# The inverse standard deviation of every LayerNorm taken from ScalarE and VectorE and given to GpSimd as a power of -0.5

## The chip, the cores and the metric

The kernel runs on one core of a Trainium2 chip. The metric is the time of one launch on the device in microseconds (us); of the kernel before, three runs were timed. One further execution was taken with the hardware profiler, and every duration below is from that one. The engines are named as in the profile: PE is TensorE (the matrix unit; PEld is its loading of weights), DVE is VectorE, ACT is ScalarE, POOL is GpSimd, and SP is SyncE, which only issues DMAs here. POOL issues DMAs too, from the same queue of instructions in which its arithmetic stands.

## The reference

Four graph layers over the same adjacency matrix of 3327 x 3327. Each adds its output to its input and normalizes every row of 512.

```python
def _layernorm(x, axis=-1, eps=1e-5):
    m = mean(x); v = var(x)
    return (x - m) / sqrt(v + eps)
# layers 0, 2 and 3: graph attention with 8, 8 and 4 heads (elu behind layers 2 and 3)
Wh = h @ W                                    # (n, H, D), H * D = 512
e = leaky_relu(s1[i] + s2[j], 0.2)            # s1, s2: Wh times two vectors, per head
att = softmax over j of where(adj > 0, e, -9e15)
h_prime = att @ Wh
# layer 1: mean of the first 64 neighbours, two linear layers with leaky_relu, added
x = _layernorm(x + layer(x, adj))             # four times
```

What matters here is the last line: 3327 rows of 512 are normalized four times, and no scale or shift follows.

## The kernel before

Rows are cut into 26 tiles of 128 (the last one has 127 rows, and `valid` zeroes its surplus row). A tile lies with a row on each partition, so the mean and variance of its rows are a column of 128 numbers, and the factors of a LayerNorm are computed on tiles of 128x1 or 128x2 elements.

`norm_rows` (L146) does one LayerNorm for one or two tiles. DVE computes statistics (`bn_stats` L152, `bn_aggr` L153), giving mean and variance in `mv`. ACT takes the square root of the variance plus `eps` into `rs[:, :, 0]` (L154), DVE takes its reciprocal (L155) and, at L158, makes minus the mean times it into `rs[:, :, 1]`. ACT then applies both in one pass over the 512 columns (L161). ACT evaluates functions from a table that holds some of them at a time; where the next function is in another set, an `ACT_TABLE_LOAD` stands ahead of it. The profile writes this load under the line of the instruction that needs it. The kernel's other functions on ACT are the exponential (L189, L278, L318, L1442, L1499), the sigmoid (L413) and plain copies and scalings.

`finish_steps` (L165) is the end of an attention layer for two tiles, cut into steps so that a caller can spread them: load the sums `h` from DRAM (buffer `hd`) and the layer's input `xr`, divide by the softmax's denominator (`divide`, L182), for layers 2 and 3 the elu (exponential L189 on ACT, L197 and L198 on DVE, which also add `xr`), and then `norm_rows`. In `load`, `h` goes by the queue that the caller names, and `xr` by POOL's; the DMAs of both have line 126, in `load_tile`.

The launch passes through these stages, in order of time:

- projection of layer 0 and building of the adjacency mask, to about 160 us; attention of layer 0, to about 950 (matmuls L855 and L811, DVE L833, ACT L834). The last groups of layer 0's LayerNorm overlap the next stage.
- layer 1, called sage, from about 950 to 1607 us. Its first part (L1185 to L1203) normalizes layer 0's output tile by tile and multiplies by the two weight matrices; weight tiles `wn` and `wl` come by POOL's queue, and L1193 is the first matmul that uses `wn`. Its second part accumulates neighbours' sums (L1295, 1352 matmuls) and, for each finished tile, runs `output` (L1270): a load `xi` by POOL (L1272), three DVE operations, `norm_rows` for this one tile, a store, and the projection for layer 2 (transposition L267, matmuls L277, exponential L278). POOL also issues the loads of counts `cy` (L1123).
- attention of layer 2, to about 2398 us, by the same code as layer 0.
- `third` (L1331), about 2398 to 2541 us: layer 2's finish, groups of two tiles, together with the projection for layer 3. A group's loads are issued three groups ahead; the first two loaded here take `h` by POOL, the others by SP. A tile's output is stored to `x3` by SP, transposed (L267), copied by ACT (L268) and multiplied (L277). In the middle of it come layer 3's preparation (L315 on DVE, L318 on ACT, transposition L324) and pieces of layer 2's sums (stores `hd`, loads `pes` L967). POOL clears two buffers, `sden` (L254) and `sm` (L256), for layer 3.
- attention of layer 3, first half of the rows (2541 to 2866 us), then second half (2868 to 3211 us), each in four units (matmuls L470, DVE L408, ACT L413). The second half carries the finish of the first half's 13 tiles as background jobs, by `finish_steps`, and a finish of its own that is written out apart: statistics into `mv`, a square root over seven tiles at once in `slots` (L1488), the factors in `scale` (L1470 reciprocal, L1471 product), applied by ACT (L1477) or DVE (L1479), then the store (L133).
- a tail, 3211 to 3229 us, with the last two groups of four and two tiles: the loop at L1523 to L1530 takes square roots at L1526 and calls `scale` for the group before.

PE's instructions run in the order in which the program writes them. The order of the other engines' and queues' instructions is chosen by a scheduler from a cost model, save for instructions that are wrapped in `keep_in_program_order`, which stay in written order relative to each other. So a change of the operation can also move other instructions on an engine. [...]

Of the kernel before, what the change touches and what calls it, by code (L numbers as in the profile page):

```python
# [7 lines left out]
F32 = mybir.dt.float32  # L8
# [4 lines left out]
AF = mybir.ActivationFunctionType  # L13
ALU = mybir.AluOpType
# [4 lines left out]
P = 128  # L19
LN_EPS = 1e-5  # L20
# [12 lines left out]
def kernel(  # L33
# [10 lines left out]
    nc = tc.nc  # L44
# [21 lines left out]
    const = ctx.enter_context(tc.tile_pool(name="const", bufs=1))  # L66
# [15 lines left out]
    for g in range(4):  # L82
# [6 lines left out]
    nc.gpsimd.memset(onecol[:, 31:32], 1.0)  # L89
    below0 = const.tile([P, 1], F32, name="below0")  # L90
    nc.gpsimd.memset(below0, -200.0)
    eps = const.tile([P, 1], F32, name="eps")
    nc.gpsimd.memset(eps, LN_EPS)
    valid = const.tile([P, 1], F32, name="valid")
    nc.gpsimd.memset(valid, 1.0)
    nc.gpsimd.affine_select(out=valid, in_=valid, compare_op=ALU.is_gt, fill=0.0, base=LAST,
                            pattern=[[0, 1]], channel_multiplier=-1)

    c1 = const.tile([P, 2, 16], F32, name="c1")
    c1a = const.tile([P, 2, 4], F32, name="c1a")  # L100
    iv = ident.rearrange("p (x c) -> p x c", c=8)
# [17 lines left out]
    def load_tile(dst, src, t, eng):  # L119

        if src.shape[0] == N and t == NT - 1 and LAST < P:
            nc.gpsimd.memset(dst, 0.0)
            for a, z in _row_pieces(LAST):
                eng.dma_start(out=dst[a:z, :], in_=src[t * P + a:t * P + z, :])
        else:
            eng.dma_start(out=dst, in_=src[t * P:(t + 1) * P, :])
# [16 lines left out]
            eng.dma_start(out=t[:, :, e, :FW], in_=src[:, e * FW:(e + 1) * FW].rearrange("(c p) m -> p c m", p=P))  # L143


    def norm_rows(pool, ys, t0):  # L146
        n = len(ys)
        st = pool.tile([P, 4, 6], F32, name="st")
        mv = pool.tile([P, 4, 2], F32, name="mv")
        rs = pool.tile([P, 4, 2], F32, name="rs")  # L150
        for s, y in enumerate(ys):
            nc.vector.bn_stats(out=st[:, s, :], in_=y)  # L152
            nc.vector.bn_aggr(out=mv[:, s, :], in_=st[:, s, :])  # L153
        nc.scalar.activation(rs[:, :n, 0], mv[:, :n, 1], AF.Sqrt, bias=eps)  # L154
        nc.vector.reciprocal(rs[:, :n, 0], rs[:, :n, 0])  # L155
        if t0 + n == NT:
            nc.vector.tensor_tensor(rs[:, n - 1, 0:1], rs[:, n - 1, 0:1], valid, op=ALU.mult)
        nc.vector.scalar_tensor_tensor(rs[:, :n, 1], mv[:, :n, 0], -1.0, rs[:, :n, 0],  # L158
                                       op0=ALU.mult, op1=ALU.mult)
        for s, y in enumerate(ys):  # L160
            nc.scalar.activation(y, y, AF.Identity, bias=rs[:, s, 1:2], scale=rs[:, s, 0:1])  # L161
# [3 lines left out]
    def finish_steps(pool, xin, layer, t0, n, hbufs=6, eng=nc.sync, xbufs=None, xpool=None, ebufs=None, pinned=False,  # L165
                     together=False):
        H, D = layer.H, layer.D
        ys, xs, steps = [], [], []

        def load():  # L170
            for t in range(t0, t0 + n):
                xr = xpool.tile([P, F], F32, name="xr", tag="hb") if xpool else \
                    pool.tile([P, F], F32, name="xr", bufs=xbufs)
                h = pool.tile([P, F], F32, name="h", bufs=hbufs)
                load_tile(h, hd, t, eng)
                ys.append(h)
                load_tile(xr, xin, t, nc.gpsimd)
                xs.append(xr)

        def divide(s):  # L180
            h = ys[s]
            ins = nc.vector.tensor_tensor(h.rearrange("p (h d) -> p h d", h=H), h.rearrange("p (h d) -> p h d", h=H),  # L182
                                          rec[:, t0 + s, :H].rearrange("p (h e) -> p h e", e=1).to_broadcast([P, H, D]),
                                          op=ALU.mult)
            if pinned and t0 > 2:
                tc.keep_in_program_order(ins)
            if layer.elu:
                e = pool.tile([P, F], F32, name="e", bufs=ebufs)
                ins = nc.scalar.activation(e, h, AF.Exp)  # L189
                if pinned and layer.li == 2 and (t0, s) == (2, 0):  # L190
                    tc.keep_in_program_order(ins)
                xs.append(e)

        def add(s):
            h, xr = ys[s], xs[s]
            if layer.elu:
                nc.vector.scalar_tensor_tensor(xr, xs[n + s], 1.0, xr, op0=ALU.min, op1=ALU.add)  # L197
                nc.vector.scalar_tensor_tensor(h, h, 0.0, xr, op0=ALU.max, op1=ALU.add)  # L198
            else:
                nc.vector.tensor_tensor(h, h, xr, op=ALU.add)  # L200

        steps.append(load)
        if pinned or together:
            steps += [lambda s=s: divide(s) for s in range(n)] + [lambda s=s: add(s) for s in range(n)]
        else:
            for s in range(n):
                steps += [lambda s=s: divide(s), lambda s=s: add(s)]
        steps.append(lambda: norm_rows(pool, ys, t0))
        return ys, steps

# [1120 lines left out]
    def third(first):  # L1331
        with tc.tile_pool(name="col3", bufs=1) as cp:
# [5 lines left out]
            with tc.tile_pool(name="p_w", bufs=1, reuse_waits="tile") as wp, \  # L1338
# [23 lines left out]
                for t0 in range(0, NT, 2):  # L1362
# [4 lines left out]
                    for s, y in enumerate(ys):  # L1367
                        t = t0 + s
# [22 lines left out]
            with tc.tile_pool(name="f3", bufs=2) as fp, tc.tile_pool(name="f4", bufs=1) as gp:  # L1391
                g = gp.tile([P, HALF, F], F32, name="g")
                st = gp.tile([P, HALF, 2, 6], F32, name="st4")
                mv = gp.tile([P, HALF, 2], F32, name="mv4")
                rs = gp.tile([P, HALF, 2], F32, name="rs4")
# [71 lines left out]
                def scale(q0, n, keep, every):  # L1467
                    def factors():
                        qs = slice(q0, q0 + n)
                        keep(nc.vector.reciprocal(rs[:, qs, 0], rs[:, qs, 0]))  # L1470
                        keep(nc.vector.scalar_tensor_tensor(rs[:, qs, 1], mv[:, qs, 0], -1.0, rs[:, qs, 0],  # L1471
                                                            op0=ALU.mult, op1=ALU.mult))

                    def one(q):
                        y = g[:, q, :]
                        if q % every == 1:
                            keep(nc.scalar.activation(y, y, AF.Identity, bias=rs[:, q, 1:2], scale=rs[:, q, 0:1]))  # L1477
                        else:
                            keep(nc.vector.tensor_scalar(y, y, rs[:, q, 0:1], rs[:, q, 1:2], op0=ALU.mult, op1=ALU.add))  # L1479
                        store(y, HALF + q, q)  # L1480

                    return [factors] + [lambda q=q: one(q) for q in range(q0, q0 + n)]

                def slots(q0, n, pt, e):
                    keep = tc.keep_in_program_order if e == 1 else lambda ins: ins
                    qs = slice(q0, q0 + n)
                    if e == 2:
                        return [lambda: nc.scalar.activation(rs[:, qs, 0], mv[:, qs, 1], AF.Sqrt, bias=eps)] + \  # L1488
                            scale(q0, n, keep, 3)
                    y = g[:, qs, (NS - 1) * P:]  # L1490
                    h = fp.tile([P, 4, P], F32, name="h", bufs=2)
# [31 lines left out]
                for k, (q0, n, parts) in enumerate(lasts):  # L1523
                    for f in parts[2:]:
                        f()
                    keep(nc.scalar.activation(rs[:, q0:q0 + n, 0], mv[:, q0:q0 + n, 1], AF.Sqrt, bias=eps))  # L1526
                    if k > 0:
                        for f in scale(*lasts[k - 1][:2], keep, 2):
                            f()
# [191 lines left out]
```

## Time and profile before

| | |
|---|---|
| three runs | 3236.37, 3238.24, 3240.77 us |
| median | 3238.24 us |
| profiled execution, own time | 3230.94 us |
| its span, first to last instruction | 3229.1 us |
| PE busy, share | 3137.4 us, 97% |
| DVE busy, share | 2626.5 us, 81% |
| ACT busy, share | 2295.1 us, 71% |
| POOL busy, share | 266.6 us, 8% |
| table loads at L154 | 45, 57.7 us |
| square roots at L154 | 59, 17.4 us |
| reciprocals at L155 | 59, mean 0.163 us |

The shares are of the span. A group's row in the profile gives the line, the engine, the operation, the tiles it writes and reads, how often it ran, its busy time and the mean length of one, and then the idle time of its engine just before it with what ended most of that. A row of the timeline gives start and length, the instruction, and in brackets how long its engine had been idle before it and for what. "Granted clock" (PEclk) is the share of full speed at which PE was allowed to run; its mean over the span was 0.987.

### The profile page before, as it was taken

Reading aid. Unit: us, or ns where it says so; the run is one execution under the profiler, and the core shown is the slowest. Engines: PE = TensorE matmul, PEld = TensorE weight load, DVE = VectorE, ACT = ScalarE, POOL = GpSimd, SP = SyncE. Lnnn points to the kernel's source line nnn. Section 1 sums busy time; section 2 is a strip of 40 time slices with the busy share of each in tenths; the row PEclk is TensorE's granted clock in tenths of the full one; section 3 lists DMA queues with packets and bytes.
Section 4 is the critical chain, followed back from the end, with each engine's and each line's share of the span. In section 5 each row is a group of like instructions: output and inputs, shape, how many; then the busy total and the mean of one; then the engine's idle time right before and its main releaser. Section 6 shows DMA issues by size and latency. Waiting matters only on the chain. (4 is left out here: it accounts for less than half of the span.)

```text
span 3229.1 us, 44980 instructions
## 1 busy us (share of the span) xinstructions
PE 3137.4 (97%) x17910; PEld 1602.3 (50%) x17910; DVE 2626.5 (81%) x2316; ACT 2295.1 (71%) x1855; POOL 266.6 (8%) x414
## 2 busy tenths in 40 slices
PE   8899999999999999999999999999989999999997
PEld 7643343333334467777744333333347655555444
DVE  5799999999987655555499999999999666677887
ACT  1388888899883234444398988899988655568896
POOL 3110000000000111111220000000011000010110
PEclk9999999999999999999999999999999999999998
DMA  9742113111024345555441111011137211122212
GB/s 360 272 149 80 41 51 137 59 45 42 25 87 138 104 127 133 134 142 152 120 135 42 41 35 39 20 42 42 32 107 242 85 43 43 43 59 89 85 47 69
DMA packets 358321, 301.80 MB, mean 93 GB/s; under 512 B 232756, under 2 KB 291966, under 8 KB 356575
## 3 DMA queue, kind: packets, MB, share of 16 engines
q1 hardware_dynamic: 325727, 187.73, 19.9%
q0 software_dynamic: 26864, 103.50, 10.0%
q10 hardware_dynamic: 5520, 7.69, 0.7%
q8 instruction: 142, 2.33, 0.3%
q14 instruction: 68, 0.56, 0.1%
HBM read 221.97 MB, written 76.84 MB: 93 GB/s over the span
## 5 line engine op out<-in xcount | busy, mean ns | idle before, releaser
L834 ACT ACTIVATE y<-t,bi,sc 128x3328 fp8e4<-128x3328 f32 (+1 forms) x520 | 1336.9, 2604 | 100.0 <-PE pd L811 47.8
L855 PE MATMUL po<-t,vj 128*64 128x448 f32 (+1 forms) x6656 | 1272.9, 522 | 14.6 <-DVE t L833 14.5
L855 PEld LDWEIGHTS po<-t,vj 128*64 128x64 f32 x6656 | 461.0, 137 | 687.8 <-issue 617.6
L470 PE MATMUL po<-t,vj 128*128 128x448 f32 (+1 forms) x1456 | 523.3, 516 | 6.2 <-DVE ob L500 3.6
L408 DVE SCALAR_TENSOR_TENSOR t<-rba,qc,mk 128x1664 f32<-128x1664 f32 (+2 forms) x234 | 408.2, 1753 | 127.7 <-PE po L470 88.2
L413 ACT ACTIVATE y<-t,bi,sc 128x1664 fp8e4<-128x1664 f32 (+2 forms) x234 | 374.3, 1617 | 182.5 <-DVE t L408 170.8
L470 PEld LDWEIGHTS po<-t,vj 128*128 128x128 f32 x1456 | 272.1, 190 | 241.5 <-issue 149.8
L833 DVE SCALAR_TENSOR_TENSOR t<-rba,qc,mask 128x3328 f32<-128x3328 f32 (+1 forms) x130 | 381.1, 2987 | 5.7 <-PE po L855 4.9
L833 DVE SCALAR_TENSOR_TENSOR t<-rbb,qc,mask 128x3328 f32<-128x3328 f32 (+1 forms) x130 | 379.9, 2982 | 6.8 <-PE po L855 3.2
L833 DVE SCALAR_TENSOR_TENSOR t<-rbb,qc,mk 128x3328 f32<-128x3328 f32 (+1 forms) x130 | 379.2, 2981 | 6.7 <-PE po L855 4.5
L833 DVE SCALAR_TENSOR_TENSOR t<-rba,qc,mk 128x3328 f32<-128x3328 f32 (+1 forms) x130 | 379.7, 2986 | 5.7 <-PE po L855 3.4
L1295 PE MATMUL acc<-zs,kt 128*128 128x512 f32 x1352 | 360.2, 420 | 0.0
L277 PE MATMUL pw<-wsb,xT 128*128 128x264 f32 (+1 forms) x1248 | 301.7, 397 | 8.8 <-DVE vt L283 7.3
L1295 PEld LDWEIGHTS acc<-zs,kt 128*128 128x128 f32 x1352 | 256.0, 190 | 51.8 <-PE pk L1146 0.8
L811 PE MATMUL pd<-y,sden 128*32 128x384 fp8e4 (+1 forms) x3328 | 270.2, 343 | 0.0
L277 PEld LDWEIGHTS pw<-wsb,xT 128*128 128x128 f32 x1248 | 242.1, 197 | 50.9 <-issue 6.5
L1153 ACT CAST pk<-cy 128x512 f32<-128x512 bf16 x169 | 99.1, 587 | 222.6 <-DVE kt L1167 216.1
L1167 DVE SCALAR_TENSOR_TENSOR kt<-pk,mb 128x512 fp32r<-128x512 f32 x169 | 115.5, 684 | 115.4 <-PE pk L1164 114.2
L811 PEld LDWEIGHTS <-sden 128*32 128x32 bf16 x3328 | 89.1, 95 | 165.3 <-issue 149.9
L283 DVE TENSOR_TENSOR vt<-pw,dc 128x256 f32<-128x256 f32 x156 | 58.7, 417 | 70.5 <-ACT dc L278 64.7
L1193 PE MATMUL pz<-wn,xT 128*128 128x512 f32 x208 | 96.0, 605 | 5.9 <-DMA wn<-in_wnT_dram 5.5
L1123 POOL DMA_DIRECT2D cy<-ctd x91 | 68.0, 747 | 371.1 <-ACT pk L1153 304.7
(249 smaller groups left out, 2234.2 us busy)
## 6 DMA issues: line engine op xcount, KB each, us to landing
raw<-in_adjT_dram SPq DMA_DIRECT2D x67, 416.0 KB
vj<-v SPq DMA_DIRECT2D x169, 128.0 KB
cy<-ctd POOLq DMA_DIRECT2D x78, 256.0 KB, 4.3
h<-hd SPq DMA_DIRECT2D x61, 256.0 KB
v<-vt SPq DMA_DIRECT2D x50, 256.0 KB
xr<-x POOLq DMA_DIRECT2D x45, 256.0 KB, 3.2
md<-mask SPq DMA_DIRECT2D x26, 416.0 KB
mb<-md SPq DMA_DIRECT2D x169, 64.0 KB
```

Source lines behind the costliest of these rows:

```text
L277: nc.tensor.matmul(pw[e][:, :FW + H], xT[:, c, :], wsb[:, c, e, :], start=c == 0, stop=c == FC - 1)
L408: ins = nc.vector.scalar_tensor_tensor(t[:, :w], rb[:, lo:lo + w], self.qc[:, j, h:h + 1], mask_at[0](j, i0 + lo, w), op0=ALU.max, op1=ALU ...
L413: nc.scalar.activation(y[:, :w], t[:, :w], AF.Sigmoid, bias=self.bi[:, j, h:h + 1], scale=self.sc[:, j, h:h + 1], saturate=False)
L470: nc.tensor.matmul(po[c][k * D:(k + 1) * D, :z - a_], vj[:, j % 2, k * D:(k + 1) * D], ts[k][:, a_:z], start=j == 0, stop=j == NT - 1)
L811: nc.tensor.matmul(pd[c][32 * kk:32 * kk + 32, :w_], lhsT, rhs, start=(kk, c) not in seen, stop=last and j == NT - 1)
L833: nc.vector.scalar_tensor_tensor(to, ro, self.qc[:, j, h:h + 1], m, op0=ALU.max, op1=ALU.mult)
L834: nc.scalar.activation(yo, to, AF.Sigmoid, bias=self.bi[:, j, h:h + 1], scale=self.sc[:, j, h:h + 1], saturate=False)
L855: nc.tensor.matmul(po[c][k * D:(k + 1) * D, :z - a_], vj[:, j % 2, x_:x_ + D], t[:, k, a_:z], start=j == 0, stop=j == NT - 1)
L1153: nc.scalar.copy(pks[k % 2], carry[b, t // 4 * 4][:, t % 4:t % 4 + 2, :])
L1167: nc.vector.scalar_tensor_tensor(kt, pk, NEIGHBOURS, mb[:, t:t + 2, :], op0=ALU.is_le, op1=ALU.mult)
L1193: nc.tensor.matmul(pz, xT[:, c, :], wn[:, c, :], start=c == 0, stop=c == FC - 1)
L1295: nc.tensor.matmul(acc, kts[b, t][:, s * P:(s + 1) * P], zs(t, c), start=t == 0 and c == 0, stop=t == NT - 1 and c == 1)
```

## The change

A helper `rsqrt` replaces the square root on ACT and the reciprocal on DVE by two instructions on POOL: the addition of eps to the variance, and a power with the exponent -0.5, read from a constant tile `power` that takes the place of the tile `eps`. It is used at all places: in `norm_rows` (59 executions, 32 of them on 128x2 and 27 on 128x1 elements), and in the last half's own finish (128x7, 128x4 and 128x2). The roots in the tail were pinned in written order and their replacements are not. One more edit goes with it: in the finish of layer 2, within and just ahead of `third`, the loads of `xr` go by SP's queue and no longer by POOL's; there are 26 of them, of 256 KB each.

```diff
--- before.py
+++ after.py
@@ -89,13 +89,13 @@
     nc.gpsimd.memset(onecol[:, 31:32], 1.0)
     below0 = const.tile([P, 1], F32, name="below0")
     nc.gpsimd.memset(below0, -200.0)
-    eps = const.tile([P, 1], F32, name="eps")
-    nc.gpsimd.memset(eps, LN_EPS)
     valid = const.tile([P, 1], F32, name="valid")
     nc.gpsimd.memset(valid, 1.0)
     nc.gpsimd.affine_select(out=valid, in_=valid, compare_op=ALU.is_gt, fill=0.0, base=LAST,
                             pattern=[[0, 1]], channel_multiplier=-1)
 
+    power = const.tile([P, 8], F32, name="power")
+    nc.gpsimd.memset(power, -0.5)
     c1 = const.tile([P, 2, 16], F32, name="c1")
     c1a = const.tile([P, 2, 4], F32, name="c1a")
     iv = ident.rearrange("p (x c) -> p x c", c=8)
@@ -143,6 +143,11 @@
             eng.dma_start(out=t[:, :, e, :FW], in_=src[:, e * FW:(e + 1) * FW].rearrange("(c p) m -> p c m", p=P))
 
 
+    def rsqrt(out, var):
+        n = out.shape[-1]
+        return [nc.gpsimd.tensor_scalar(out, var, LN_EPS, None, op0=ALU.add),
+                nc.gpsimd.tensor_tensor(out, out, power[:, :n], op=ALU.pow)]
+
     def norm_rows(pool, ys, t0):
         n = len(ys)
         st = pool.tile([P, 4, 6], F32, name="st")
@@ -151,8 +156,7 @@
         for s, y in enumerate(ys):
             nc.vector.bn_stats(out=st[:, s, :], in_=y)
             nc.vector.bn_aggr(out=mv[:, s, :], in_=st[:, s, :])
-        nc.scalar.activation(rs[:, :n, 0], mv[:, :n, 1], AF.Sqrt, bias=eps)
-        nc.vector.reciprocal(rs[:, :n, 0], rs[:, :n, 0])
+        rsqrt(rs[:, :n, 0], mv[:, :n, 1])
         if t0 + n == NT:
             nc.vector.tensor_tensor(rs[:, n - 1, 0:1], rs[:, n - 1, 0:1], valid, op=ALU.mult)
         nc.vector.scalar_tensor_tensor(rs[:, :n, 1], mv[:, :n, 0], -1.0, rs[:, :n, 0],
@@ -174,7 +178,7 @@
                 h = pool.tile([P, F], F32, name="h", bufs=hbufs)
                 load_tile(h, hd, t, eng)
                 ys.append(h)
-                load_tile(xr, xin, t, nc.gpsimd)
+                load_tile(xr, xin, t, nc.sync if layer.li == 2 else nc.gpsimd)
                 xs.append(xr)
 
         def divide(s):
@@ -1467,7 +1471,6 @@
                 def scale(q0, n, keep, every):
                     def factors():
                         qs = slice(q0, q0 + n)
-                        keep(nc.vector.reciprocal(rs[:, qs, 0], rs[:, qs, 0]))
                         keep(nc.vector.scalar_tensor_tensor(rs[:, qs, 1], mv[:, qs, 0], -1.0, rs[:, qs, 0],
                                                             op0=ALU.mult, op1=ALU.mult))
 
@@ -1485,7 +1488,7 @@
                     keep = tc.keep_in_program_order if e == 1 else lambda ins: ins
                     qs = slice(q0, q0 + n)
                     if e == 2:
-                        return [lambda: nc.scalar.activation(rs[:, qs, 0], mv[:, qs, 1], AF.Sqrt, bias=eps)] + \
+                        return [lambda: rsqrt(rs[:, qs, 0], mv[:, qs, 1])] + \
                             scale(q0, n, keep, 3)
                     y = g[:, qs, (NS - 1) * P:]
                     h = fp.tile([P, 4, P], F32, name="h", bufs=2)
@@ -1523,7 +1526,7 @@
                 for k, (q0, n, parts) in enumerate(lasts):
                     for f in parts[2:]:
                         f()
-                    keep(nc.scalar.activation(rs[:, q0:q0 + n, 0], mv[:, q0:q0 + n, 1], AF.Sqrt, bias=eps))
+                    rsqrt(rs[:, q0:q0 + n, 0], mv[:, q0:q0 + n, 1])
                     if k > 0:
                         for f in scale(*lasts[k - 1][:2], keep, 2):
                             f()
```

## The prediction

> **What bounds the kernel now.** I read the page's first part, then the busy tenths by slice, then ACT's and POOL's groups, then PE's waits, then the timeline at the places that these point to.
>
> ```profile
> PE 3137.4 (97%) x17910; PEld 1602.3 (50%) x17910; DVE 2626.5 (81%) x2316; ACT 2295.1 (71%) x1855; POOL 266.6 (8%) x414
> PE   8899999999999999999999999999989999999997
> ```
>
> TensorE is busy 3137.4 of 3229.1 us. A change that leaves its instructions as they are, as this one does, can win at most the 91.7 us in which it idles, and only where a norm ends the idling. The one weak slice in the middle is the 31st, about 2420 to 2500 us: layer 3's projection, with layer 2's finish in it. ACT, from which the work is taken, is no bound as a whole; what of it matters is the place.
>
> ```profile
> L154 ACT ACT_TABLE_LOAD x45 | 57.7, 1283 | 41.3 <-DVE mv L153 40.8
> L278 ACT ACT_TABLE_LOAD x33 | 42.3, 1283 | 0.6
> L154 ACT ACTIVATE rs<-mv,eps 128x2 f32<-128x2 f32 (+1 forms) x59 | 17.4, 295 | 17.3 <-DVE mv L153 16.6
> ```
>
> ACT reloads its function table 45 times for a square root (L154) and 33 times to go back for the exponential of L278. Of POOL's groups this is the nearest to the operation that is added, elementwise, but 156 wide:
>
> ```profile
> L384 POOL TENSOR_SCALAR sm<-pc 128x156 bf16<-128x156 bf16 x14 | 17.4, 1291 | 54.7 <-ACT pc L372 30.7 <-DVE pc L372 24.0
> ```
>
> ```profile
> PE pt L267 <- ACT h L161: 11.8, 4, 8.3
> PE pr L324 <- ACT rc L318: 4.3, 1, 4.3
> ```
>
> Of PE's waits (total, times, longest) only the first names a norm: 11.8 us in four waits, one of 8.3. The timeline places both big ones at the start of the third stage:
>
> ```profile
> 2402.06 1.28 ACT L154 ACT_TABLE_LOAD   x1
> ...
> 2403.35 0.30 ACT L154 ACTIVATE rs<-mv,eps 128x2 f32<-128x2 f32 x1
> ...
> 2405.55 0.16 DVE L155 RECIPROCAL rs<-rs 128x2 f32<-128x2 f32 x1
> ...
> 2408.36 0.69 DVE L182 TENSOR_TENSOR h<-h,rec 128x512 f32<-128x512 f32 x1 [2.65 <-DMA h<-hd]
> ...
> 2408.97 0.15 DVE L158 SCALAR_TENSOR_TENSOR rs<-mv,rs 128x2 f32<-128x2 f32 x1
> ...
> 2410.03 1.97 PE L267 MATMUL pt<-ident,h 128*128 128x128 f32 x8 [8.29 <-ACT h L161]
> ...
> 2416.23 2.01 POOL L254 MEMSET sden<- 128x2288 bf16 x1 [13.55 <-DMA hd<-hb]
> ...
> 2422.86 1.36 PE L267 MATMUL pt<-ident,h 128*128 128x128 f32 x8 [2.55 <-ACT h L161]
> ```
>
> The root was ready at 2403.65, but the reciprocal stood on DVE behind three L182 multiplications, and L158 behind one more that waited 2.65 us for a load. The table load is a minor part of this wait; the place in DVE's queue is the major one.
>
> **What the Trainium skill says.** "ScalarE: Activation LUTs", section "What ACT_TABLE_LOAD costs", puts a switch at about 1.28 us of load and 1.38 us of drain. The trace agrees on the load (1283 ns, every one) and shows no drain behind it: the square root starts 1.29 us after the load did. I price a load at 1.28. "GPSIMD Engine Reference", section "Elementwise — side-by-side cycle accounting", gives about 2.6 cycles an element for two inputs, and no price for a power; at 2 elements the start of the instruction must dominate, so it doesn't settle the price. Its section "Instruction dispatch" says that a Pool instruction that needs the one before must wait on a semaphore, so add and pow don't overlap. "Trainium Kernel Development and Optimization", section "Key Constraints", has DMAs of all issuing queues share the same 16 engines: moving loads to SP saves issue time alone. The trace agrees as far as it goes (541 ns an issue on POOL, 0.37 to 0.58 on SP in this stage).
>
> **The change part by part.**
>
> *Removed from ACT.* 62 square roots (59 at L154, one at L1488, two at L1526) of about 0.295 us: 18.3 us. The order of instructions of the built kernel has 61 table loads for 145 before: 84 fewer by 1.283 are 107.8 us. The 61 left are switches between exponential and sigmoid at L413, L189 and L1442, which no norm causes. In all 126 us of ACT, which by itself is worth nothing.
>
> *Removed from DVE.* 62 reciprocals by 0.163 us: 10 us.
>
> *Added to POOL.* 124 instructions of 1 to 8 columns. No row of before shows pow, or an add this small. From below: the 128x1 memset, 0.095 us, and a 128x1 affine select, 0.185. From above: L384's 1.29 us at 156 columns. I take 0.4 each and 0.9 for the pair with its semaphores; the bounds for the pair are 0.3 and 2.6. The old way from the last statistics to L158 took 2.4 us with a load (1312.58 to 1314.96) and 0.56 without one (976.29 to 976.85). The new way thus wins 1.5 us where a load was, loses 0.3 where none was, and at the upper bound loses in both.
>
> *Moved.* 26 loads of xr, 256 KB each, go from POOL's to SP's queue in the third stage.
>
> By stage:
>
> 1. Up to 950 us, in layer 2's attention (1615 to 2398) and in layer 3's first half (2541 to 2866) there are no norms but those that overlap the next stage: 0.
> 2. Start of sage, 955 to 963 us: POOL's new pair stands ahead of the load of wn, for which PE waits 5.5 us (L1193). Loss 0.5 (0 to 1.5).
> 3. Sage's accumulation, 1160 to 1600 us: some 46 of the 84 loads go here, and PE is busy 439.6 of 440 us. Its matmuls hide everything: 0 (without that cover 46 loads would be 59 us). The one memset for the exponents takes the place of that for eps: 0. Were POOL slow, the pair stands between the load L1272 and the next L1123; at 1311 to 1315.5 us it has 3 us of slack.
> 4. End of sage, 1604 to 1608 us: the last tile's add stands behind a 3.91 us memset (L254, to 1604.5) and its pow behind another of 1.48 (L256). PE waits 3.6 us here for the projection that needs this norm. About 0.5 lost (0 to 1.5).
> 5. Third stage, 2398 to 2541 us. PE idles about 20 us in it. In the new order of DVE two L182 stand ahead of L158 where more stood before; the first norm's L161 ends near 2405.5 instead of 2410: 4.5 won. The second wait (2.55 us, with several slower tiles ahead of it) goes in part, which makes about 5.5 in all by the second group, or 2 if the pow is held behind L254's memset, which before waited 13.55 us for a store. L318's wait of 4.3 us gets 2 from its lost table load and an earlier reduction on DVE; smaller waits give 1. Against that, DVE has only 8.5 us idle in 2400 to 2480 plus the reciprocals' 1.5, and is what comes late next. DMA is busy 0.80 of those 80 us at 256 GB/s, so the h loads, not the norms, may set the pace. SP gets about 9 issues for two tiles by 0.38 us, 3.4 of 7.9 us: it keeps up, but the xr loads also stand among stores that wait for DVE. Together 6.5 won (loss of 2 to gain of 10).
> 6. Layer 3's second half, 2868 to 3211 us: its units take 83 to 84 us for 79.7 in the first half, ACT is busy 212.4 of 240 us in 2880 to 3120, PE idles some 6. 13 table loads (16.7 us) and ten roots (3 us) go. Few of PE's waits there belong to a norm: L408, L500 and L669 on DVE make up most. Taken: 3 won (0 to 8).
> 7. Tail, after 3215 us: the last norm's chain is root at 3220.56, reciprocal at 3221.73. A pair of under 1.1 us on POOL wins 0.3, one of 2 us loses 1.3. Taken: 0.
>
> Sum: 0.5 + 0.5 - 6.5 - 3 = 8.5 us won, with a little more from waits that DVE's reciprocals end: I call it 9. The profiled execution took 3230.9 us (span 3229.1), 7.3 below the median of the runs, 3238.24; it would take about 3222, and the median becomes 3229.
>
> A measurement of this kernel can tell 0.2%, 6.5 us, from no change.
>
> **The rivals.**
>
> - *Hidden anyway.* DVE (36.4 of 40 us busy in 2440 to 2480) and the DMA take over at once, and the second half stays bound by its sigmoid and exponential switches. For it: PE's waits name a norm for 11.8 us alone. Against: the 8.3 us wait is plainly one of order. It gives 3234 to 3240.
> - *Slower: POOL's queue.* POOL executes in order, and the pair stands behind memsets, DMA issues and instructions that wait for stores. In the third stage each of 13 groups needs its pair before its projection. It decides once pair and place cost more than the 2.4 us of the old way: at 3.4 us, 13 groups lose 13 us, of which DVE's slack of 8.5 hides part, and the tail another 2; SP's xr loads coming late would look alike. It gives about 3248. For it: 13.55 us of waiting ahead of L254. Against: POOL is busy 8%, and its other queue entries in this stage go to SP.
> - *Larger.* The second half's units fall from 83.5 toward 80, since 19.7 us of ACT work are gone where ACT is 88% busy: 10 won instead of 3. It gives about 3221.
> - *Doesn't do what it says.* The loads might stay because exponential, sigmoid and square root still alternate. The built order excludes it for 84 of them.
>
> **How the numbers follow.** Forecast (5 to 12 us won) 0.48; larger 0.20; hidden 0.14; slower by POOL or SP 0.18. The forecast's own range is 3226 to 3233, and the likeliest time is 3229. The 8-in-10 range takes in larger, hidden and the nearer part of slower: 3215 to 3244. Of the forecast a tenth falls within 6.5 us, and so does nearly all of hidden and a little of slower. Faster by over 0.2%: 0.64; within: 0.19; slower: 0.17.
>
> **What would show it.** In the profile after: no load at L154, about 61 loads in all, ACT near 2170 us, POOL near 320; PE's first matmul of the third stage 4 to 5 us closer to the end of layer 2's attention; a unit of the second half about 1 us shorter; sage's 440 us unchanged. Wrong would be the sum if PE waits at L267 with a releaser on POOL, if the pow's rows show over 1 us, or if DVE waits for xr from SP at L197.

## The result and the profile after

The changed kernel takes 3226.96 us (median of 5 runs, 3222.80 to 3228.25), the kernel before 3238.24 (median of 5, 3236.37 to 3240.77). The ratio is 0.9962, with a 95% interval of 0.9948 to 0.9977: 11.3 us faster. The profiled execution of after took 3224.4 us (span 3222.7).

The page of after, its first part and PE's busy tenths:

```profile
PE 3134.4 (97%) x17910; PEld 1597.5 (50%) x17910; DVE 2618.7 (81%) x2254; ACT 2176.2 (68%) x1709; POOL 318.8 (10%) x512
PE   8899999999999999999999999999998999999997
```

ACT lost 118.9 us, with 61 table loads left of 145, and PE did the same work in a span that is 6.4 us shorter. Behind the new helper (L146 to L149) this kernel's line numbers are 4 higher than before, at its end 3 higher; the kernels of the experiments have their own. POOL's groups show the two new operations (count, busy time, mean ns, then POOL's idle time before them):

```profile
L149 POOL TENSOR_TENSOR rs<-rs,power 128x2 f32<-128x2 f32 (+3 forms) x62 | 42.4, 684 | 4.9
...
L148 POOL TENSOR_SCALAR rs<-mv 128x2 f32<-128x2 f32 (+3 forms) x62 | 19.2, 309 | 249.0 <-DVE mv L158 168.2 <-DVE mv L1512 73.9 <-ACT rr L330 6.8
```

An add of 0.31 us and a power of 0.68 make a pair of 1.0, about 1.1 with the step between them.

Where the time went is read from first and last starts of a few matmuls. These are the rows of the attention matmuls (source view: minimum, median and maximum ns, then first and last start), before and after:

```profile
L855 PE MATMUL po<-t,vj x6656: 485/538/1009, 143.4 to 2396.9; 128*64 128x448 f32 x100, 128*64 128x384 f32 x96
...
L470 PE MATMUL po<-t,vj x1456: 485/512/644, 2535.7 to 3115.2; 128*128 128x448 f32 x182
```

```profile
L859 PE MATMUL po<-t,vj x6656: 486/539/1009, 142.4 to 2404.2; 128*64 128x448 f32 x100, 128*64 128x384 f32 x96
...
L474 PE MATMUL po<-t,vj x1456: 486/512/643, 2537.0 to 3110.2; 128*128 128x448 f32 x182
```

The third stage is the stretch from the last L855 to the first L470: 138.8 us before, 132.8 after. Layer 3's two halves are the stretch of L470: 579.5 before, 573.2 after. Outside the quoted rows all lines are named as in the kernel before. The same stretches, taken from the profiles of all kernels of this study:

| kernel | third stage | layer 3 (L470) | first L1185 to first L1193 | first L1193 to first L1295 | last L669 to end |
|---|---|---|---|---|---|
| before | 138.8 | 579.5 | 6.9 | 196.7 | 18.5 |
| after | 132.8 | 573.2 | 4.7 | 199.8 | 20.5 |
| e1 moved xr loads alone | 135.8 | 582.4 | 6.8 | 197.6 | 20.6 |
| e2 power, xr not moved | 136.2 | 573.2 | 5.2 | 200.6 | 18.6 |
| e3 layer 2 alone, xr moved | 132.6 | 582.1 | 6.6 | 196.7 | 21.0 |
| e4 layer 3 alone | 139.4 | 573.2 | 6.8 | 196.9 | 18.2 |
| e5 layers 0 and 1 alone | 139.1 | 582.2 | 4.4 | 199.5 | 18.7 |
| e6 slower pair | 147.8 | 577.8 | 6.3 | 206.8 | 23.6 |
| e7 roots back on ACT, layer 3 | 132.9 | 574.0 | 4.3 | 199.8 | 20.4 |
| e10 layers 2 and 3, xr moved | 131.6 | 573.1 | 6.9 | 196.6 | 20.3 |
| e11 roots back on ACT, layer 2 | 139.8 | 573.2 | 5.2 | 199.2 | 20.3 |
| e12 roots and reciprocals back, layer 3 | 133.4 | 573.9 | 4.5 | 199.4 | 20.6 |
| e13 roots and reciprocals back, layer 2 | 140.4 | 573.2 | 5.0 | 199.0 | 20.3 |
| e14 before, three h buffers | 139.1 | 578.5 | 6.8 | 196.7 | 18.6 |

What isn't touched by the change repeats within about 1 us in four of these columns. Layer 3 with its old norms spreads over 578.5 to 582.4 us. That is the granted clock, which was at half speed there for 3.4 to 6.8 us in some of these executions and never in others. The same goes for the whole: layer 2's attention, which the change doesn't touch, took 796.7 us in the profile of before and 802.4 in that of after, with 10.2 and 23.9 us at half clock. This is a part of why the two profiled executions differ by 6.5 us only and the medians by 11.3.

So a stretch can get shorter in two ways: PE idles less, or it works at full clock for longer. These rows tell them apart (windows view: stretch, its length, PE's busy time; the first figure behind POOL's instructions is the mean granted clock); they are the third stage of before, after, e1 and e2:

```profile
2396.90:2535.70 138.80, 119.25 (x582) 98.93 (x579) 112.83 (x263) 105.99 (x217) 20.61 (x38) 0.93 0.64 209
```

```profile
2404.20:2537.00 132.80, 117.50 (x583) 97.49 (x580) 110.33 (x250) 70.02 (x179) 22.68 (x40) 0.96 0.66 223
```

```profile
2397.00:2532.80 135.80, 116.86 (x583) 97.60 (x580) 112.12 (x263) 105.63 (x218) 8.75 (x14) 0.95 0.65 218
```

```profile
2400.60:2536.80 136.20, 120.51 (x582) 99.69 (x579) 110.50 (x250) 70.11 (x179) 35.94 (x64) 0.94 0.64 213
```

and layer 3 before and after:

```profile
2535.70:3115.20 579.50, 572.20 (x2423) 302.01 (x2423) 421.93 (x358) 403.42 (x284) 35.88 (x62) 1.00 0.22 61
```

```profile
2537.00:3110.20 573.20, 571.42 (x2424) 301.85 (x2422) 423.79 (x352) 397.95 (x274) 44.40 (x76) 1.00 0.22 61
```

PE's idle time is length less busy time. For all kernels, with the time at half clock from the clock's record in each trace (us):

| kernel | third stage: PE idle | at half clock | layer 3: PE idle | at half clock |
|---|---|---|---|---|
| before | 19.5 | 20.5 | 7.3 | 0 |
| after | 15.3 | 10.2 | 1.8 | 0 |
| e1 | 18.9 | 13.7 | 7.3 | 6.8 |
| e2 | 15.7 | 17.1 | 1.8 | 0 |
| e3 | 15.0 | 10.2 | 6.9 | 6.8 |
| e4 | 20.0 | 23.9 | 1.8 | 0 |
| e5 | 19.3 | 20.5 | 7.0 | 6.8 |
| e6 | 28.1 | 17.1 | 4.5 | 3.4 |
| e7 | 15.0 | 10.2 | 2.3 | 0 |
| e10 | 15.1 | 10.2 | 1.8 | 0 |
| e11 | 20.7 | 17.1 | 1.8 | 0 |
| e12 | 15.3 | 13.7 | 2.3 | 0 |
| e13 | 21.0 | 17.1 | 1.8 | 0 |
| e14 | 20.0 | 20.5 | 5.2 | 3.4 |

Of the 6.0 us of the third stage, 4.2 are idle time and the other 1.8 are PE's own work, which was at half clock for half as long. The time at half clock goes with the kernel there (20.5 to 23.9 us in the four whose third stage is as before, 10.2 to 13.7 in the five that have the power and the moved loads there and nothing put back there), but each is one execution, and no run isolates the clock. Of layer 3's 6.3 us, 5.5 are idle time.

The start of the third stage after, to be held against the lines of the prediction (timeline: start, length, instruction, idle time before it):

```profile
2411.07 0.23 POOL L148 TENSOR_SCALAR rs<-mv 128x2 f32<-128x2 f32 x1 [4.21 <-DVE mv L158]
2411.39 0.73 POOL L149 TENSOR_TENSOR rs<-rs,power 128x2 f32<-128x2 f32 x1
...
2412.42 0.15 DVE L162 SCALAR_TENSOR_TENSOR rs<-mv,rs 128x2 f32<-128x2 f32 x1
...
2413.47 1.97 PE L271 MATMUL pt<-ident,h 128*128 128x128 f32 x8 [4.38 <-ACT h L165]
...
2419.11 2.00 POOL L258 MEMSET sden<- 128x2288 bf16 x1 [7.00 <-DMA hd<-hb]
...
2422.78 0.72 POOL L149 TENSOR_TENSOR rs<-rs,power 128x2 f32<-128x2 f32 x1
...
2424.59 1.36 PE L271 MATMUL pt<-ident,h 128*128 128x128 f32 x8 [0.58 <-ACT h L165]
```

Layer 2's attention ended at 2404.2 here (2396.9 before). So the first transposition came 9.3 us behind it (13.1 before), the third tile's 20.4 (26.0 before). PE's waits in the third stage after (total, times, longest):

```profile
PE pt L271 <- ACT h L165: 13.2, 8, 4.4
...
PE pr L328 <- ACT rr L330: 0.2, 1, 0.2
```

The wait for the normalized tile is no shorter in sum than before (11.8), but spread over eight places; of the transposition L324's wait of 4.3 us, 0.2 are left, and this is about what PE idles less.

### The profile page after: what moved, and what is told of

It is laid out like the page before. It is cut to its first block, busy times and chain, and to the rows that moved or that the text cites. A ratio compares the mean times of both kernels' runs of the same rounds, so it can differ in the third digit from the quotient of the medians.

```text
span 3222.7 us, 44966 instructions
## 1 busy us (share of the span) xinstructions
PE 3134.4 (97%) x17910; PEld 1597.5 (50%) x17910; DVE 2618.7 (81%) x2254; ACT 2176.2 (68%) x1709; POOL 318.8 (10%) x512
## 3 DMA queue, kind: packets, MB, share of 16 engines
q1 hardware_dynamic: 329471, 194.55, 20.6%
## 5 line engine op out<-in xcount | busy, mean ns | idle before, releaser
L165 ACT ACTIVATE h<-h,rs 128x512 f32<-128x512 f32 x65 | 49.5, 806 | 70.3 <-DVE rs L162 70.3
```

## The experiments

The norm's way was made selectable by layer, so that each kernel below differs from before or after in the place named. Each time is a median, with its ratio to the runs of before on the same chip.

**e1, the moved loads alone.**

```diff
-                load_tile(xr, xin, t, nc.gpsimd)
+                load_tile(xr, xin, t, nc.sync if layer.li == 2 else nc.gpsimd)
```

> The kernel before, with nothing changed but the 26 loads of xr in layer 2's finish, which go by SP's queue. Theory 1 (the norm's chain makes the gain of the third stage, and the freed ACT that of layer 3): the third stage, from the last matmul L855 to the first L470, stays at 138.8 us within 2 us, and the time is that of before within 0.1%. Rival (the moved loads free POOL's queue, and this is what wins the third stage): the third stage falls to about 133 us and the time by about 6 us.

Measured: 3233.85 us, ratio 0.9989 (0.9982 to 0.9995). The third stage took 135.8 us: half of the gain in time, which theory 1 had not allowed. In that stage DVE waited 2.3 us for h at L182, for 5.3 before: with both loads in SP's queue, h and xr alternate, where POOL had issued five xr loads in a row at 2399.54. PE's first wait there shrank from 8.3 to 6.7 us. But over the stage PE idled only 0.6 us less than before (18.9 for 19.5); the rest of the 3.0 us is PE's work, at half clock for 13.7 us and not 20.5. Whether the moved loads cause that too is not shown. The tail after the last L669 grew by 2.1 us.

**e2, the power without the moved loads.**

```diff
-                load_tile(xr, xin, t, nc.sync if layer.li == 2 else nc.gpsimd)
+                load_tile(xr, xin, t, nc.gpsimd)
```

> The whole change, but the loads of xr stay in POOL's queue. Theory 1: the third stage keeps most of its 6 us (134 to 136 us for 132.8 of the whole change), and the time is within 3 us of the whole change. Rival (a pair behind DMA issues on POOL comes too late for PE): the third stage goes back to 138 us or more, PE waits at the transposition L267 for more than 16 us, and the time is 5 us or more above the whole change.

Measured: 3227.70 us, ratio 0.9973 (0.9962 to 0.9984). The third stage took 136.2 us. So the power alone wins about 2.6 us there, the moved loads alone 3.0, and both 6.0: in time they add. In PE's idle time they don't share alike: the power alone takes 3.8 us off it, the moved loads alone 0.6, both 4.2. The tail is 18.6 us, as before; the 2 us come with the moved loads in every kernel that has them (20.3 to 21.0, against 18.2 to 18.7 without, the slowed pair of e6 apart).

**e3, layer 2 alone.** Every norm but layer 2's goes back to square root and reciprocal; the xr loads are moved.

```diff
-        rsqrt(rs[:, :n, 0], mv[:, :n, 1])
+        if li == 2:
+            rsqrt(rs[:, :n, 0], mv[:, :n, 1])
+        else:
+            nc.scalar.activation(rs[:, :n, 0], mv[:, :n, 1], AF.Sqrt, bias=eps)
+            nc.vector.reciprocal(rs[:, :n, 0], rs[:, :n, 0])
```

> The power on POOL, with the moved xr loads, in layer 2's norms alone; layers 0, 1 and 3 keep square root and reciprocal. Theory 1: the third stage takes 133 us as with the whole change, layer 3 (first to last matmul L470) 579 us as before, sage as before; the time is 5 to 6 us below before. Rival (the stages are not separate, for instance the third stage's gain needs the removed loads elsewhere): the third stage stays at 137 us or more.

Measured: 3227.67 us, ratio 0.9968 (0.9958 to 0.9979); third stage 132.6 us. The stage's gain needs nothing from the others. The time fell by more than the stage explains, and by more than the 5 to 6 us expected: 10.7 us, where the stage gives 6.2 and the tail takes 2. The interval is some 7 us wide, and what the rest is stays open.

**e4, layer 3 alone.** The same edit with `li == 3`, and the power in the last half's own finish; xr by POOL.

> The power on POOL in layer 3's norms alone (first half's finish, the last seven tiles' and the tail); layers 0 to 2 keep square root and reciprocal, xr by POOL. Theory 1: layer 3 from first to last matmul L470 takes 573 us for 579.5 before, the third stage 138 to 139 as before, and the time is about 6 us below before, or 4 if the tail's 2 us more come from the power too. Rival (layer 3's shorter time follows from what the third stage leaves behind): 579 us as before.

Measured: 3227.36 us, ratio 0.9967 (0.9954 to 0.9980); layer 3 took 573.2 us, the third stage 139.4. So layer 3's gain is its own, and about as large as that of the third stage. The time fell by 11.0 us, where 6 were expected. With e3's 10.7 the parts would add up to more than e10, which has both (15.6): the medians are too coarse for the parts, and the argument rests on the stretches.

**e5, layers 0 and 1 alone.** The same edit with `li < 2`.

> The power on POOL in the norms of layers 0 and 1 alone (25 + 46 of the table loads removed lie here); layers 2 and 3 keep square root and reciprocal, xr by POOL. Theory 1: the 48 loads removed win nothing, and the pair costs a little where no load stood before: from the first L1193 to the first L1295 about 200 us for 196.7 before, from the first L1185 to the first L1193 about 5 for 6.9, from the first to the last L1295 441 to 442 for 440.7; the time is 0 to 3 us above before. Rival (the loads removed count even beside a full PE): the accumulation L1295 gets shorter and the time is 5 us or more below before.

Measured: 3234.96 us, ratio 0.9992 (0.9984 to 1.0000). The first L1193 came 2.5 us earlier, and the rest of sage's first part took 2.8 more; the accumulation, first to last L1295, took 441.1 us for 440.7. From 1160 to 1605 us ACT had 48 table loads before and has 1 here: 47 loads gone beside a full PE win nothing there (the "25 + 46" of the expectation is a slip; 49 loads go in this kernel). The time is 1.8 us below before, where 0 to 3 above were expected; the interval reaches to no change.

**e6, a slower pair.**

```diff
+    ones8 = const.tile([P, 8], F32, name="ones8")
+    nc.gpsimd.memset(ones8, 1.0)
...
         nc.gpsimd.tensor_tensor(out, out, power[:, :n], op=ALU.pow)
+        nc.gpsimd.tensor_tensor(out, out, ones8[:, :n], op=ALU.pow)
+        nc.gpsimd.tensor_tensor(out, out, ones8[:, :n], op=ALU.pow)
```

> The whole change with two more powers (exponent 1, which leave the value) behind each pair on POOL, in all 62 places: the pair of 1.1 us becomes about 2.9 us. It asks from which price POOL decides. Theory 1: the third stage has 13 groups and little slack, so it takes 137 to 142 us for 132.8; the first part of sage loses 5 to 8 us more; layer 3 keeps its 573 us within 1; the tail is 3 us longer; the time is 8 to 20 us above the whole change. Rival (POOL's part lies beside other work): the time is within 4 us of the whole change, nearly all of it the tail.

Measured: 3265.08 us, ratio 1.0092 (1.0078 to 1.0106), 28 us slower than before and 38 slower than after. The first norm of its third stage (timeline):

```profile
2422.82 0.23 POOL L153 TENSOR_SCALAR rs<-mv 128x2 f32<-128x2 f32 x1 [4.08 <-DVE mv L170]
2423.13 0.73 POOL L154 TENSOR_TENSOR rs<-rs,power 128x2 f32<-128x2 f32 x1
2423.94 1.10 POOL L155 TENSOR_TENSOR rs<-rs,ones 128x2 f32<-128x2 f32 x1
2425.12 0.69 POOL L156 TENSOR_TENSOR rs<-rs,ones 128x2 f32<-128x2 f32 x1
2425.84 0.16 DVE L174 SCALAR_TENSOR_TENSOR rs<-mv,rs 128x2 f32<-128x2 f32 x1 [1.35 <-POOL rs L156]
```

From the add's start to DVE's product 3.0 us pass, for 1.35 in after. The third stage pays 15.0 us for it in 13 groups, sage's first part 7.0 (and 1.6 ahead of L1193), layer 3 4.6 (of it 2.7 in PE's idle time), the tail 3.1. That is far more than expected (137 to 142 us in the third stage, layer 3 within 1 us, 8 to 20 in all). POOL is 12% busy in this kernel. Taken as a straight line between 132.8 us at 1.35 and 147.8 at 3.0, the third stage would be back at its 138.8 with 2.0 us from add to product, and at the 135.8 of e1, which has the old norm and the moved loads, with 1.7: an estimate from these kernels.

**e7, layer 3's roots back on ACT, unread.**

```diff
         rsqrt(rs[:, :n, 0], mv[:, :n, 1])
+        if li == 3:
+            spare = pool.tile([P, 4], F32, name="spare")
+            nc.scalar.activation(spare[:, :n], mv[:, :n, 1], AF.Sqrt, bias=eps)
```

> The whole change, and in layer 3's seven norms of the first half ACT computes the square root as well, into a tile that nobody reads: 7 roots and some 14 table loads come back to ACT (about 20 us of it), while the chain of the norm still goes over POOL. Theory 1a (layer 3 gained from the freed ACT): from first to last L470 579 us again, and the time 4 to 7 us above the whole change. Theory 1b (it gained from the shorter chain, or from DVE's order): 573 to 575 us.

Measured: 3224.11 us, ratio 0.9966 (0.9954 to 0.9979). ACT's groups in layer 3's second half have the roots' loads again, and the matmuls of layer 3 take 574.0 us all the same (source view):

```profile
L172 ACT ACT_TABLE_LOAD x7 | 9.0, 1283 | 0.1
```

```profile
L487 PE MATMUL po<-t,vj x1456: 486/512/643, 2538.4 to 3112.4; 128*128 128x448 f32 x182
```

With the returns to the other sets, 12 more loads than in after stand in that stretch (52 for 40; before had 46). In layer 3 PE idles 2.3 us, for 1.8 in after and 7.3 before. Theory 1a falls: layer 3 didn't gain from what ACT was freed of.

**e10, layers 2 and 3.** The edit of e3 with `li >= 2`, the power in the last half's own finish, xr moved.

> The power on POOL in the norms of layers 2 and 3 with the moved xr loads, square root and reciprocal kept in layers 0 and 1, where no stage gained. Theory 1: from the first L1193 to the first L1295 197 us as before, the third stage 133, layer 3 from first to last L470 573; the time is 2 to 3 us below the whole change, 13 to 15 below before. Rival (parts don't add): the time of the whole change or above.

Measured: 3221.20 us, ratio 0.9953 (0.9941 to 0.9965). It is faster than before by 15.6 us. Against the whole change (0.9948 to 0.9977) the intervals overlap, so that it beats after isn't shown; the stages favour it by 1.0 us at sage's start (6.9 + 196.6 for 4.7 + 199.8) and 1.2 in the third stage.

**e11 and e13, layer 2's roots, and roots with reciprocals, back unread.** As e7 with `li == 2`; e13 adds one line.

```diff
+            nc.vector.reciprocal(spare[:, :n], spare[:, :n])
```

> The whole change, and in layer 2's 13 norms ACT computes the square root as well, into a tile that nobody reads; 13 roots and about 20 table loads come back to ACT in the third stage, the chain of the norm still goes over POOL. Theory 2a (the third stage gained from a shorter chain of the norm, ACT having room): 132 to 134 us from the last L855 to the first L470. Theory 2b (it gained from ACT's lost table loads): 136 us or more, as with the moved loads of xr alone (135.8).

> As the run before, and DVE also takes the reciprocal of ACT's unread root, ahead of the product L158, so that DVE waits for ACT as it did in the kernel before, and the norm with it. Theory 2a: 135 us or more in the third stage, since DVE's queue now stands at the old wait. Rival (what gained is the moved place of DVE's other work, which this leaves): 132 to 134 us.

Measured: 3226.77 us, ratio 0.9975 (0.9966 to 0.9984), for e11; 3229.80, ratio 0.9979 (0.9972 to 0.9985), for e13. The third stage took 139.8 and 140.4 us, although the norm itself still went over POOL and stayed short: in e11's first group 1.8 us pass from the last statistics to the end of the product, for 1.6 in after and 6.3 before. Among PE's waits in e11's third stage are these:

```profile
PE pw L294 <- ACT spare L172: 3.7, 1, 3.7
PE pw L294 <- ACT xT L285: 2.5, 2, 1.3
```

Neither wait is in after. ACT copies every transposed tile (L268) for PE, and the copies stand behind the loads in its queue: 30 loads in this stage before and in e11, 4 in after. PE idles 5.4 us more than in after; the other 1.6 us of the 7.0 are work at half clock. Theory 2b holds here, by the profiles of two kernels: the times of the whole, whose intervals overlap that of after, don't resolve 7 us. The reciprocal adds 0.6 us, which is not clear of the spread. In e13 too the scheduler put it behind the product (2416.44 us, the product at 2414.97), so DVE did not wait for ACT ahead of it, and e13 doesn't test what it was made for.

**e12, layer 3's roots and reciprocals back, unread.** As e13 with `li == 3`.

> The whole change, and in layer 3's seven norms of the first half both root (ACT) and reciprocal (DVE) come back unread, the latter ahead of the product L158, so that the norm's end hangs on ACT again. Theory 3 (layer 3 gained because the norm ends earlier, so that its two h buffers are stored, freed and loaded again before DVE asks for them): 577 to 580 us from first to last L470, and DVE's waits for h at L182 above 8 us again. Rival (the gain is the pace of ACT or the order of the queues): 573 to 575 us.

Measured: 3224.46 us, ratio 0.9964 (0.9950 to 0.9977); layer 3 took 573.9 us. The scheduler put each reciprocal behind the product and one step of attention, so the norm did not hang on ACT again, and the run doesn't decide what it was made for. It shows that the reciprocals as work on DVE cost layer 3 nothing either (573.9 us for the 574.0 of e7).

**e14, a third h buffer in the kernel before.**

```diff
-                            ys, steps = finish_steps(fp, x3, L3, t0, min(2, HALF - t0), 2, together=True)
+                            ys, steps = finish_steps(fp, x3, L3, t0, min(2, HALF - t0), 3, together=True)
...
-                    h = fp.tile([P, 4, P], F32, name="h", bufs=2)
+                    h = fp.tile([P, 4, P], F32, name="h", bufs=3)
```

(the second edit at both places of that line)

> The kernel before with three h buffers for two in layer 3's second half[...], square root and reciprocal as before. Theory 3: one tile of each next pair comes before the last pair is stored, so DVE's waits for h (12.8 us at L182 before) fall below 6 us, and the time from first to last L470 to 575 to 577 us for 579.5, the whole 2 to 5 us below before. Rival (h is not what holds DVE): 579 us or more, the time of before.

Measured: 3233.51 us, ratio 0.9988 (0.9981 to 0.9994); layer 3 took 578.5 us, DVE's waits for h at L182 summed to 11.1. The gain of the whole is of the size expected, but the waits hardly fell: in SP's queue the loads of h still stood behind the stores of the pair before. PE idled 5.2 us in layer 3, for 6.9 to 7.3 in the four kernels with the old norm and two buffers; 3.4 us at half clock hide that in the 578.5. So the third buffer took about 2 of the 5.5 us: this speaks for theory 3, but the waits that it names did not fall as expected, and it doesn't confirm it.

## Why the prediction was right, and where not

The forecast was 3229 us; 3226.96 came out, with the 11.3 us inside the forecast's 5 to 12. The two stages that it named did win, and sage and the tail did not. But the sum came out in part by luck: in the third stage wrong steps cancelled, and layer 3's term was half of what it should have been. By its steps:

**The reading of the slices.** The weak slice in the middle of before is the 30th (2341 to 2422 us), not the 31st; it ends with the start of the third stage, where the two waits lie that the prediction then read from the timeline. The 31st is the weak one in after.

**Prices.** The pair was taken at 0.4 each and 0.9 with its semaphores, and measured 0.31 and 0.68, 1.1 together; the power started 0.09 us behind the add's end in the group shown above. The start is not nearly all of it, even at so few elements: the power took 0.57 us for one column, 0.74 for two, 1.18 for four and 1.52 for seven, which is roughly 0.16 a column over a start of 0.4 (an estimate by a straight line). The counts held: 61 table loads are left, ACT is at 2176 us (near 2170 expected), POOL at 319 (near 320).

**Sage.** The accumulation was costed at nothing, and e5 shows it. At its start a loss of 0.5 was expected, because the pair stands ahead of the load of `wn`. The sum fits, 0.9 us lost, but by two terms that were not seen: POOL's order changed so that `wn` was issued at 952.78 us for 954.37 before, and L1193 came 2.2 us earlier after the first L1185; then the rest of sage's first part took 3.1 us longer. That goes with the power in layer 0's norms (199.0 to 200.6 us in the kernels that have it, 206.8 with the slower pair of e6, 196.6 to 197.6 in those that don't). That these norms, which had had their root at hand without a load, took longer is the likely reason; no run isolates it. The end of sage lost what was expected and as expected: PE's wait went from 3.6 to 4.1 us. The last tile's statistics ended at 1605.46 us, the add started at 1606.16, when the memset ahead of it was done, and the power at 1607.78, behind the second memset.

**Third stage.** 6.5 us were expected and 6.0 came. The start was right in size (3.8 us for 4.5, then 5.6 for 5.5). L324's wait, of which 2 us were to go, went almost whole (4.1). What was gained at the start was not kept: later tiles made PE wait for the norm, in all 13.2 us for 11.8. Three steps under the sum were wrong. First, the moved loads were priced at issue time alone; that leaves out the order in which h and xr are loaded, and by measurement the stage is 3.0 us shorter in e1, though PE's waits account for 0.6 of it. Second, ACT's 126 us were said to be worth nothing by themselves, and the wait to be one of place in DVE's queue; e11 puts 26 of the stage's loads back beside a short norm and loses 7.0 us. Third, the clock was no part of the sum, and PE spent 10.2 us of the stage at half clock for 20.5 before. That these came to 6.0 and not to more or less is luck.

**Layer 3's second half.** The mis-sized term: 3 us expected, 6.3 measured between the two profiles, 5.5 of it in PE's idle time (the 9 us to e1, e3 and e5 are in part their 6.8 us at half clock). It went toward the rival called larger, which had 10, yet for another cause than that gave. It named the freed ACT, and e7 and e12 exclude that; besides, ACT lost only 8 loads in this half (54 before, 46 after), for the 13 of the forecast. What the traces show is the way of one group in the kernel before:

```profile
2932.70 0.18 DVE L153 BATCH_NORM_AGGREGATE mv<-st 128x2 f32<-128x6 f32 x1
...
2935.18 0.30 ACT L154 ACTIVATE rs<-mv,eps 128x2 f32<-128x2 f32 x1
...
2938.47 1.51 ACT L161 ACTIVATE h<-h,rs 128x512 f32<-128x512 f32 x2
...
2939.88 0.93 SPq L133 DMA_DIRECT2D out_dram<-h  x2
...
2945.46 0.95 SPq L126 DMA_DIRECT2D h<-hd  x2
...
2948.08 0.69 DVE L182 TENSOR_TENSOR h<-h,rec 128x512 f32<-128x512 f32 x1 [6.65 <-DMA h<-hd]
```

and of the like group after:

```profile
2930.11 0.17 DVE L158 BATCH_NORM_AGGREGATE mv<-st 128x2 f32<-128x6 f32 x1
...
2931.96 1.50 ACT L165 ACTIVATE h<-h,rs 128x512 f32<-128x512 f32 x2
...
2932.79 1.05 SPq L133 DMA_DIRECT2D out_dram<-h  x2
...
2934.85 0.33 SPq L126 DMA_DIRECT2D h<-hd  x1
...
2937.59 0.69 DVE L186 TENSOR_TENSOR h<-h,rec 128x512 f32<-128x512 f32 x1 [0.42 <-DMA h<-hd]
```

From the last statistics to the end of the apply 7.1 us pass before (a sigmoid, the load, the root, the load back, another sigmoid, then the apply) and 3.2 after. In the six groups of two it is 7.1 to 10.5 us before and 3.0 to 5.2 after. The two h buffers are stored and filled again only behind that, so DVE stops for the next h, with the attention's own work queued behind it. The group shown has the longest of these stops, and not for the norm alone: 5.6 us pass there from the store's issue to that of the next load, for 2.1 to 2.6 in the other groups of before; why is open. Over layer 3's second half, DVE's waits for h sum to this, before and after:

```profile
DVE h L182 <- DMA h<-hd: 12.8, 7, 6.7
```

```profile
DVE h L186 <- DMA h<-hd: 2.7, 4, 1.1
```

e6 shows that the length of this way is a cause: it only lengthens the pair, and DVE waits 5.5 us for h, and PE idles 4.5 us in layer 3. In after, e6 and before the way takes 3.2, 4.5 and 7.9 us (medians of the six groups), and PE idles 1.8, 4.5 and 7.3. That the two buffers carry it is argued from these traces: a third one gave back about 2 us (e14), and a kernel with four was not run.

**Tail.** A change of nothing was expected. The pair does nothing to it: from the last statistics to the last apply L1479 1.6 us pass before (3220.53 to 3222.12) and 1.5 after (3212.14 to 3213.65). But from the last store's issue on POOL to the end of the span it is 5.8 us before and 7.9 after:

```profile
3223.32 0.54 POOL L133 DMA_DIRECT2D out_dram<-g  x1 [0.16 <-issue]
```

```profile
3214.82 0.54 POOL L133 DMA_DIRECT2D out_dram<-g  x1 [0.16 <-issue]
```

This goes with the moved xr loads, as e1 and e2 show. The stores are not slower: the last one has landed 3.8 us after its issue in both. What is longer is POOL's closing instruction, a DRAIN that the timeline leaves out: in the traces it takes 4.8 to 5.2 us in the five kernels where POOL issues 344 DMAs, and 6.6 to 7.5 in the nine where it issues 318. Why fewer DMAs should lengthen it stays open.

**The slower rival** had its mechanism and its side right. It put the point of decision at the old way's 2.4 us from the last statistics to the product, and feared about 10 us in all at 3.4. e6 has 3.0 from add to product and loses 28, of it 9.0 in the third stage and, what the rival had not counted, 9.5 at sage's start; the estimate from it has the third stage lose from about 2 on. The pair was at 1.35.

## What to carry to other kernels

A small operation that moves to another engine is worth what it does to the queues it leaves and to the chain it stands in, and these are different in each stage: here freed table loads won nothing beside a full TensorE, 7 us where ACT's copies feed TensorE, and nothing beside layer 3's sigmoids, where the shorter way of the norm made the gain. Try each stage and each edit alone; an edit that goes along for order's sake, like the moved loads, can carry half of a stage's gain and cost part of it elsewhere. When a stretch gets shorter, look at how much of it is TensorE's idle time and how much its clock. Before a chain goes over POOL, double its price in a trial: the margin here was under a microsecond per norm.

## What was not expected of the hardware

A power with exponent 1 took about as long as that with -0.5 (means of 0.65 us for the two in e6, 0.68 for the other), and the price grows with the columns, from 0.57 us for 128x1 to 1.52 for 128x7. Moving 26 loads from POOL's queue to SP's at 2400 us lengthened the very end of the program, 800 us later, by 2 us, all of it in POOL's closing DRAIN (5.05 us before, 7.13 after). PE's clock was at half speed for 20.5 us of the third stage before and 10.2 after, which is about 1.8 us of PE's work.
